# Spreading the small products of a graph layer over TensorE's four strips, with an earlier ranking and two slot buffers

## The chip, the cores and the metric

The kernel runs on one core of a Trainium2 chip. The metric is the device time of one execution in microseconds (us): before the change the median of three runs is 540.39 us (539.81 to 543.72). The engines are named as the profile names them: PE is TensorE (PEld its weight loads), ACT is ScalarE, DVE is VectorE, POOL is GpSimd, SP is SyncE, which here only issues DMAs. "The change" is the kernel after it; line numbers are those of the kernel before, unless said otherwise.

## The reference, cut to what matters

A graph layer with 6250 nodes of 128 features and 100000 edges, sorted by their target node. Each edge has one of two types, and its message is the source row times the weight of that type. The messages are summed per target; the node's own product is added; then relu, a residual and a layer norm.

```python
Xs = X[src]                                    # 100000 x 128
m_data = Xs @ W_data.T + b_data
m_ctrl = Xs @ W_control.T + b_control
msg = jnp.where((edge_types == 0)[:, None], m_data, m_ctrl)
agg = jax.ops.segment_sum(msg, dst, num_segments=X.shape[0])
out = jax.nn.relu(agg + (X @ W_self.T + b_self))
x = _layernorm(x + out, axis=-1)               # (h - mean) / sqrt(var + 1e-5)
```

## The kernel before

**Tiles.** The products of all nodes with both message weights are made once (49 blocks of 128 nodes, each with two types: 98 columns of a table). Each is held as three bf16 parts side by side, 384 columns (`D3`), in the tile `m3`, which stays in SBUF. The targets are cut into 39 *windows* of 160 nodes (`WN`); ten nodes are left over and go through an indirect gather. Eleven *groups* of windows (`GROUPS`: 1, 2, then nine of 4) share their preparation.

**Ranking** (`ranks`, once per group). The edges of a window (22 x 124 slots) are loaded (`win`) and turned into one-hot rows (`hots`). PE counts and ranks them (L810, L846), DVE reduces the ranks (`slot`, L851), PE scatters each edge into one of 32 places per table column (L890, into the PSUM tile `vt`). DVE takes `vt` out as `vs` (L905 to L911). SP writes `vs` to DRAM (`packed`, L917), from where each window of the group is read back, spread over all partitions (`rows`, 784 KB, L1043). Edges that find no place go through a short list (L993) and a gather.

**Sums** (`sums`, once per window). DVE turns `rows` in place into one-hot columns (L1053). Then 25 *groups of strips* follow each other, g = 0 to 24. Stage one (L1075): four products with 32 columns of weights each, so that each uses one strip of 32 columns of PE and writes 32 partitions of the PSUM tile `gp`; each streams 384 columns of `m3`. They fetch up to 128 message rows. ACT or DVE copies them out of PSUM to `gs` as bf16 (L484 or L485, the function `evict`). Stage two sums them by target into the PSUM tile `a`. A window has 160 targets: 128 of them are four blocks of 32, one strip each, and stream the 384 columns of `gs` (L1092). The last 32 targets go into the columns of `a` behind the first 384 (`a[..., D3:]`): there the three parts of 128 columns are three *small products* (L1095), the part c on strip c, so on strips 0, 1 and 2. At the window's end those three blocks are copied out as `bs` (96 partitions) and added by a product with `fold` (L615), a 96 x 32 matrix of three identities.

**Finish** (`close`, once per group). DVE adds the three parts of `a` (L624), the residual and the statistics; POOL or ACT scales; SP stores. The products of L615 go into the same PSUM tile `vt` that the scatter uses (it has one buffer), and DVE reads them at L633.

**Order.** Nothing is scheduled on the chip: each engine runs its list of instructions in order. A planner (`Plan.run`) writes these lists: it goes through all operations with assumed costs (the number in `add("PE", 0.168, ...)` is such a cost, in us) and gives each engine, when it is free, the ready operation with the earliest due time. It also decides there whether an `evict` goes to ACT or DVE. The due times of `ranks` follow from `when`, which for later groups lies `LEAD` = 80 ahead of the due time of the group's first window (`T0 + w0 * TW`, 13 per window). Buffers are rings: the load of `rows` of window i may only be issued when stage one of window i - 3 has read its buffer (`B(work, [P, R, NT], BF16, "rows", 3, ...)`). Before the windows, the first three chunks of the transposed input (`xts`) use the same three buffers.

Of the kernel before, what the change touches and what calls it, by code (L numbers as in the profile page):

```python
# [10 lines left out]
F32 = mybir.dt.float32  # L11
BF16 = mybir.dt.bfloat16
# [9 lines left out]
P = 128  # L22
D = 128
D3 = 3 * D
# [14 lines left out]
WN = 160  # L39
# [5 lines left out]
R = 32  # L45
W4 = WN - P
NT = 2 * NB
NS = 25
# [218 lines left out]
def sums_over_windows(ctx, tc, x, xt, edges, w, bias, out, total):  # L267
    nc = tc.nc
    V, A, G, T, S = nc.vector, nc.scalar, nc.gpsimd, nc.tensor, nc.sync
# [6 lines left out]
    add = plan.add  # L276
# [5 lines left out]
    def B(pool, shape, dtype, name, bufs=1, room=None):  # L282
        return Buf(plan, pool, shape, dtype, name, bufs, room)

    def C(shape, dtype, name):
        return Buf(plan, const, shape, dtype, name, 1)

    XC = 4 * WN
    T0 = 36.0
    DOUBLE = ('lo1', 'to1', 'slot2', 'pay', 'inside', 'unit')  # L290
    TW = 13.0
# [32 lines left out]
    def vec(due, cols, fn, r, w, rate=1.04):  # L324
        return add("DVE", dve(cols, rate), fn, due, r, w)

    def vp(on_pool, due, cols, fn, r, w, rate=1.04, slow=1.0):
# [57 lines left out]
    fold = C([3 * R, R], F32, "fold")  # L385
    vec(30, R, lambda: V.tensor_add(fold.t, ident.t[: 3 * R, 0:R], ident.t[: 3 * R, R : 2 * R]),
        [ident], [fold])
    vec(30, R, lambda: V.tensor_add(fold.t, fold.t, ident.t[: 3 * R, 2 * R : 3 * R]),
        [ident, fold], [fold])
# [115 lines left out]
    for j, n in enumerate(XB):  # L505
        ring = ("rows", 3, R * NT) if j < 3 else ("hot2", 2, NS * WN)
        xts.append(B(work, [D, 2 * n * P], BF16, *ring))
# [208 lines left out]
    def ranks(gi, w0, nw, when, late, step, engines):  # L716
# [140 lines left out]
        for ci, (k0, k1) in enumerate(zip(cs, cs[1:])):  # L857
# [36 lines left out]
            add("PE", .25 + m * 0.0275, scatter, dc + 1, [(two, 0), (two, 1)] + hkeys(k0, k1), [vt])  # L894
# [136 lines left out]

    def sums(gi, w0, nw, placed):
# [5 lines left out]
        for i in range(nw):  # L1038
            due = T0 + (w0 + i) * TW
            sp = B(work, [P, R, NT], BF16, "rows", 3, R * NT)  # L1040
# [27 lines left out]
            for g in range(NS):  # L1068
# [4 lines left out]
                def stage1(g=g, gp=gp, sp=sp, last=last):  # L1073
                    for t in range(2 if last else 4):
                        T.matmul(gp.t[R * t : R * t + R, :D3], sp.t[:, :, 4 * g + t],  # L1075
                                 m3.t[:, 4 * g + t, :], start=True, stop=True)
                s1.append(add("PE", 0.168, stage1, d, [sp] + m3_key(g), [gp]))
# [12 lines left out]
                def stage2(g=g, gs=gs, a=a, hot2=hot2, last=last):  # L1090
                    for j in range(4):
                        T.matmul(a.t[R * j : R * j + R, :D3], hot2.t[:, g, R * j : R * j + R],  # L1092
                                 gs.t, start=g == 0, stop=False, skip_group_check=True)
                    for c in range(3):
                        T.matmul(a.t[R * c : R * c + R, D3:], hot2.t[:, g, P:],  # L1095
                                 gs.t[:, c * D : (c + 1) * D], start=False, stop=last,
                                 skip_group_check=True)
                s2.append(add("PE", 0.178, stage2, d + 0.9, [gs, (hot2, sum(g >= c for c in cuts[1:-1]))], [a]))
# [6 lines left out]
            bs = B(work, [3 * R, D], F32, "bs", 5)  # L1105
            evict(lambda bs=bs: bs.t, lambda a=a: a.t[: 3 * R, D3:], D, due + TW + 0.8, [a], [bs]).slack = 0.25
# [86 lines left out]
    for gi, nw in enumerate(GROUPS):  # L1193
        if gi == 0:
            when, late, step, engines = 0.0, 12.0, 0.5, ["SP"]
        elif gi == 1:
            when, late, step, engines = 8.0, 14.0, 0.6, ["SP", "ACT"]
        else:
            span = nw * TW
            when = max(when + late + 22 * step + GAP, T0 + w0 * TW - LEAD)  # L1200
            late, step, engines = LF * span, SF * span, ["SP"]
        todo.append((gi, w0, nw, when, late, step, engines))
        w0 += nw
# [170 lines left out]
```

## Time and profile before

| | |
|---|---|
| median of three runs | 540.39 us (539.81 to 543.72) |
| the profiled execution | 542.22 us, its span 540.4 us |
| granted TensorE clock, mean | 0.983 |
| PE busy | 502.1 us (93%), 13288 products |
| PEld busy | 432.6 us (80%) |
| DVE busy | 441.1 us (82%) |
| ACT busy | 429.0 us (79%) |
| POOL busy | 201.5 us (37%) |

Three stretches make up the span: the message products until about 62 us, the 39 windows until about 528 us, and a tail that closes the last group. In the views, a line reads: source line, engine, operation, names of output and inputs (buffer numbers left out), shapes, count, then busy time and mean duration, then idle time of that engine before it and what ended it. Instructions of an engine overlap, so the union of their times is less than count times duration, and a busy PE is not PE at its peak. `g` and `x` are the PSUM tiles of stage one, `a` that of stage two.

### The profile page before, as it was taken

The page shows a single profiled execution, that of the slowest core. Times are in us where ns is not written, and L with a number is a line of the kernel's source. Part 1 is how long each engine was busy: PE and PEld are TensorE (multiplying, and loading weights), DVE is VectorE, ACT ScalarE, POOL GpSimd, SP SyncE. Part 2 cuts the span into 40 slices and gives each one's busy share as a digit, 9 for nine tenths or more (in the row PEclk, how much of TensorE's full clock was granted, in tenths as well). Part 3 has the DMA queues.
Part 4 walks back from the last instruction along what each step waited for, and adds up shares of the span by engine and source line. Part 5 has one row for each costly group of instructions (what it writes and reads, how often), then busy time and mean ns, then how long its engine had stood idle before and what let it go on. Part 6 is the DMA issues. An engine that isn't in the chain of part 4 may idle for free. (4 is left out here: it accounts for less than half of the span.)

```text
span 540.4 us, 30907 instructions
## 1 busy us (share of the span) xinstructions
PE 502.1 (93%) x13288; PEld 432.6 (80%) x13288; DVE 441.1 (82%) x1168; ACT 429.0 (79%) x1077; POOL 201.5 (37%) x284
## 2 busy tenths in 40 slices
PE   7799879799999988999999999999999999999991
PEld 4465557699889877888988887888898899888990
DVE  6388989889989997898989889979978678956642
ACT  4566767698889877888988878978898898878990
POOL 1000535700830684176067247707701720542000
PEclk9989899999999998999999999999999999999997
DMA  7466661540453055325413533351342352234200
GB/s 244 160 256 224 240 181 29 167 161 6 134 145 88 12 139 151 98 77 152 141 38 111 141 95 95 91 180 41 115 128 88 115 163 89 63 107 126 70 19 17
DMA packets 44932, 63.43 MB, mean 117 GB/s; under 512 B 19178, under 2 KB 35279, under 8 KB 44751
## 3 DMA queue, kind: packets, MB, share of 16 engines
q1 hardware_dynamic: 41745, 56.22, 33.5%
q0 software_dynamic: 1120, 2.23, 2.0%
q10 hardware_dynamic: 1922, 2.91, 1.7%
q8 instruction: 106, 1.74, 1.3%
q14 instruction: 39, 0.32, 0.2%
HBM read 45.61 MB, written 13.82 MB: 110 GB/s over the span
## 5 line engine op out<-in xcount | busy, mean ns | idle before, releaser
L1092 PE MATMUL a<-gs,hot 128*32 128x384 bf16 x3744 | 376.1, 328 | 0.4 <-issue 0.3
L484 ACT CAST gs<-g 128x384 bf16<-128x384 f32 x700 | 302.9, 492 | 64.3 <-PE g L1075 53.6
L1075 PE MATMUL g<-m,rows 128*32 128x384 bf16 x2958 | 327.1, 336 | 9.0 <-DVE rows L1053 5.7
L1075 PEld LDWEIGHTS <-rows 128*32 128x32 bf16 x3822 | 253.4, 134 | 27.7 <-DVE rows L1053 6.5
L1095 PE MATMUL a<-gs,hot 128*32 128x128 bf16 x2808 | 273.1, 220 | 2.1 <-issue 2.1
L1092 PEld LDWEIGHTS <-hot 128*32 128x32 bf16 x3900 | 206.4, 98 | 6.7 <-issue 3.1
L1095 PEld LDWEIGHTS <-hot 128*32 128x32 bf16 x2925 | 155.6, 97 | 14.1 <-issue 2.4
L1075 PE MATMUL x<-m,rows 128*32 128x384 bf16 x864 | 122.0, 335 | 0.0
L484 ACT CAST gs<-x 128x384 bf16<-128x384 f32 x199 | 98.3, 494 | 8.6 <-PE x L1075 5.7
L1061 DVE TENSOR_TENSOR hot<-iota_b,to_d 128x1920 bf16<-128x1920 bf16 (+2 forms) x85 | 93.1, 1105 | 0.1
L851 DVE TENSOR_REDUCE slot<-rk 124x8 f32<-124x400 f32 (+2 forms) x99 | 56.1, 567 | 22.3 <-PE g L1075 10.3
L674 POOL TENSOR_SCALAR xr<-xr,mv,rstd 128x128 f32<-128x128 f32 (+1 forms) x44 | 56.5, 1289 | 21.9 <-DVE rstd L651 18.4
L846 PE MATMUL rk<-hots,tri 128*32 128x400 bf16 (+1 forms) x388 | 51.3, 337 | 4.5 <-DVE slot L851 1.5
L1053 DVE TENSOR_SCALAR rows<-rows,pid 128x3136 bf16<-128x3136 bf16 (+1 forms) x46 | 41.6, 904 | 5.7 <-DMA rows<-packed 5.7
L937 POOL TENSOR_SCALAR pv<-slot 124x88 f32<-124x88 bf16 x9 | 9.5, 1058 | 79.6 <-DVE slot L868 74.2
L624 DVE TENSOR_REDUCE s<-a 128x128 f32<-128x384 f32 (+1 forms) x40 | 22.1, 551 | 15.7 <-ACT bs L484 9.9
L1016 POOL DMA_INDIRECT sr<-table,at x20 | 29.8, 1489 | 10.8 <-DVE at L1004 6.2
L491 POOL COPY to_d<-vs 32x100 bf16<-32x100 bf16 (+1 forms) x72 | 29.2, 406 | 5.9 <-DVE vs L911 2.7
L846 PEld LDWEIGHTS <-tri 128*32 128x32 bf16 x428 | 22.9, 96 | 9.9 <-issue 8.6
L803 DVE TENSOR_TENSOR hots<-hots,val 124x1200 bf16<-124x1200 bf16 (+3 forms) x42 | 28.0, 675 | 0.0
L799 DVE TENSOR_TENSOR hots<-iota_b,st 124x1200 bf16<-124x1200 bf16 (+3 forms) x42 | 27.6, 671 | 0.0
L767 POOL TENSOR_SCALAR pay<-u 124x88 f32<-124x88 f32 x9 | 8.9, 994 | 46.2 <-DVE u L752 45.1
(224 smaller groups left out, 667.9 us busy)
## 6 DMA issues: line engine op xcount, KB each, us to landing
rows<-packed SPq DMA_DIRECT2D x36, 784.0 KB
table<-m SPq DMA_DIRECT2D x12, 768.0 KB
xc<-in_xt SPq DMA_DIRECT2D x9, 320.0 KB
rows<-packed ACTq DMA_DIRECT2D x3, 784.0 KB
rows<-in_xt SPq DMA_DIRECT2D x8, 256.0 KB
xr<-in_x SPq DMA_DIRECT2D x8, 256.0 KB
out<-xr SPq DMA_DIRECT2D x8, 256.0 KB
gl<-sr SPq DMA_DIRECT2D x39, 48.0 KB
```

Source lines behind the costliest of these rows:

```text
L484: [("ACT", act(cols), lambda: A.copy(o(), src())), ("DVE", dve(cols), lambda: V.tensor_copy(o(), src()))], None, None, due, r, w, lat)
L491: "POOL", 0.25 + cols * 0.0014, lambda: G.tensor_copy(o(), src()), due, r, w)
L674: fp = lambda k=k, m=m: G.tensor_scalar(h.t[:m, k, :], h.t[:m, k, :], mv.t[:m, k, 0:1], rstd.t[:m, k : k + 1], op0=ALU.subtract, op1=ALU.mult)
L803: vec(when + 2 + pace * k0, m * NC, lambda k0=k0, k1=k1, hs4=hs4, hp=hp: V.tensor_tensor(hp(), hp(), fl(val)[:, k0 * nw : k1 * nw, None, : ...
L846: T.matmul(acc.t[R * j : R * j + R, : (k1 - k0) * wide], tri.t[:, R * j : R * j + R], flat(k0, k1, P), start=True, stop=True, skip_group_c ...
L851: vec(due, (k1 - k0) * wide, lambda k0=k0, k1=k1, acc=acc: V.tensor_reduce(slot.t[:, k0:k1, :], acc.t[:EP, : (k1 - k0) * wide].rearrange(" ...
L1016: add("POOL", GC, lambda pr=pr, sr=sr: G.indirect_dma_start(out=sr.t[: room(pr)], out_offset=None, in_=table[:, :], in_offset=bass.Indirec ...
L1053: add("DVE", dve(half * NT, 0.305) + 0.05, lambda sp=sp, rs=rs: V.tensor_scalar(sp.t[:, rs], sp.t[:, rs], pid1.t, None, op0=ALU.is_equal), ...
L1061: lambda i=i, hot2=hot2, s4=s4, c0=c0, c1=c1: V.tensor_tensor(hot2.t[:, c0:c1].rearrange("p g (c d) -> p g c d", d=2), iota1_b.t.rearrange ...
L1075: T.matmul(gp.t[R * t : R * t + R, :D3], sp.t[:, :, 4 * g + t], m3.t[:, 4 * g + t, :], start=True, stop=True)
L1092: T.matmul(a.t[R * j : R * j + R, :D3], hot2.t[:, g, R * j : R * j + R], gs.t, start=g == 0, stop=False, skip_group_check=True)
L1095: T.matmul(a.t[R * c : R * c + R, D3:], hot2.t[:, g, P:], gs.t[:, c * D : (c + 1) * D], start=False, stop=last, skip_group_check=True)
```

## The change

Four edits.

1. **Small products on four strips.** A counter of columns per strip (`load`) is kept while the program is written. The function `turn(n, cols)` takes the n strips with the least columns so far, in that order, and adds `cols` to each. Stage one takes its four strips in the order that `turn(4, D3)` gives, stage two does so too, and the three small products go to the strips of `turn(3, D)`: any three of the four, the one that had most columns left out. The sum of the last 32 targets is then spread over four blocks of partitions, so `bs` has 128 partitions and `fold` four identities (one more addition of 32 columns on DVE, once).
2. **Further ahead.** `when` of group gi lies 4 us per group number above 4 further ahead: 4 for group 5, up to 24 for group 10.
3. **Two buffers** for `rows` in place of three. The load of a window then waits for stage one of window i - 2. The third chunk of the transposed input gets a tile of its own (`x2`).
4. **Costs of the planner.** Stage one 0.163 in place of 0.168, stage two 0.204 in place of 0.178, scatter 0.2 + 0.016 m in place of 0.25 + 0.0275 m. They cost nothing by themselves; they move instructions.

```diff
-    fold = C([3 * R, R], F32, "fold")
+    fold = C([P, R], F32, "fold")
...
     for j, n in enumerate(XB):
-        ring = ("rows", 3, R * NT) if j < 3 else ("hot2", 2, NS * WN)
-        xts.append(B(work, [D, 2 * n * P], BF16, *ring))
+        if j == 2:
+            xts.append(C([D, 2 * n * P], BF16, "x2"))
+        else:
+            ring = ("rows", 2, R * NT) if j < 2 else ("hot2", 2, NS * WN)
+            xts.append(B(work, [D, 2 * n * P], BF16, *ring))
...
-            add("PE", .25 + m * 0.0275, scatter, dc + 1, [(two, 0), (two, 1)] + hkeys(k0, k1), [vt])
+            add("PE", .2 + m * 0.016, scatter, dc + 1, [(two, 0), (two, 1)] + hkeys(k0, k1), [vt])
...
+    load = [0] * 4
+
+    def turn(n, cols):
+
+        js = sorted(range(4), key=lambda j: (load[j], j))[:n]
+        for j in js:
+            load[j] += cols
+        return js
...
-            sp = B(work, [P, R, NT], BF16, "rows", 3, R * NT)
+            sp = B(work, [P, R, NT], BF16, "rows", 2, R * NT)
...
                 def stage1(g=g, gp=gp, sp=sp, last=last):
-                    for t in range(2 if last else 4):
+                    for t in (0, 1) if last else turn(4, D3):
                         T.matmul(gp.t[R * t : R * t + R, :D3], sp.t[:, :, 4 * g + t],
                                  m3.t[:, 4 * g + t, :], start=True, stop=True)
-                s1.append(add("PE", 0.168, stage1, d, [sp] + m3_key(g), [gp]))
+                s1.append(add("PE", 0.163, stage1, d, [sp] + m3_key(g), [gp]))
...
                 def stage2(g=g, gs=gs, a=a, hot2=hot2, last=last):
-                    for j in range(4):
+                    for j in turn(4, D3):
                         T.matmul(a.t[R * j : R * j + R, :D3], hot2.t[:, g, R * j : R * j + R],
                                  gs.t, start=g == 0, stop=False, skip_group_check=True)
-                    for c in range(3):
-                        T.matmul(a.t[R * c : R * c + R, D3:], hot2.t[:, g, P:],
-                                 gs.t[:, c * D : (c + 1) * D], start=False, stop=last,
+                    for c, j in enumerate(turn(3, D)):
+                        T.matmul(a.t[R * j : R * j + R, D3:], hot2.t[:, g, P:],
+                                 gs.t[:, c * D : (c + 1) * D], start=False, stop=g > NS - 3,
                                  skip_group_check=True)
-                s2.append(add("PE", 0.178, stage2, d + 0.9, [gs, (hot2, sum(g >= c for c in cuts[1:-1]))], [a]))
+                s2.append(add("PE", 0.204, stage2, d + 0.9, [gs, (hot2, sum(g >= c for c in cuts[1:-1]))], [a]))
...
-            bs = B(work, [3 * R, D], F32, "bs", 5)
-            evict(lambda bs=bs: bs.t, lambda a=a: a.t[: 3 * R, D3:], D, due + TW + 0.8, [a], [bs]).slack = 0.25
+            bs = B(work, [P, D], F32, "bs", 5)
+            evict(lambda bs=bs: bs.t, lambda a=a: a.t[:, D3:], D, due + TW + 0.8, [a], [bs]).slack = 0.25
...
-            when = max(when + late + 22 * step + GAP, T0 + w0 * TW - LEAD)
+            when = max(when + late + 22 * step + GAP, T0 + w0 * TW - LEAD - 4 * max(gi - 4, 0))
```

Two places show how the order moves. The first is SP's queue where the group of windows 19 to 22 gets its slots: the write of `packed`, the loads of `rows` that stand behind it, and what lies between. Before, the loads are those of windows 19, 20 and 21:

```order
L917 DMA packed<-vs 128x2x98
L1043 DMA rows<-packed 128x3136
L607 DMA xb<-in_xt 128x4x32
L1043 DMA rows<-packed 128x3136
L830 DMA past<-csb 64x2x200
L833 DMA hots<-past 4x4400
L1023 DMA gl<-sr 64x384 x2
L1043 DMA rows<-packed 128x3136
```

In the change the loads are those of windows 18, 19 and 20:

```order
L921 DMA packed<-vs 128x2x98
L1056 DMA rows<-packed 128x3136
L834 DMA past<-csb 64x2x200
L837 DMA hots<-past 4x4400
L1056 DMA rows<-packed 128x3136
L611 DMA xb<-in_xt 128x4x32
L1027 DMA gl<-sr 64x384 x4
L1056 DMA rows<-packed 128x3136
```

Before, the first load behind the write reads what was just written; now a load of the group before stands between, so the write has come forward by a window against the loads. Each load now also stands behind more of the small DMAs of the ranking (`past`, `hots`, `gl`), and waits for a buffer that comes free one window later.

The second place is DVE's list where the scatter of that same group is taken out of `vt`. Before (`xr<-vt,xr` at L633 reads the products with `fold` from the same PSUM tile):

```order
L905 TENSOR_SCALAR vst<-vt 128x2x49
L982 TENSOR_SCALAR fi<-ci 124x32
L908 SCALAR_TENSOR_TENSOR vs<-vst,vt 128x98
L911 TENSOR_SCALAR vs<-vst 128x98
L982 TENSOR_SCALAR fi<-ci 124x32 x2
L633 SCALAR_TENSOR_TENSOR xr<-s,xr 128x128
L1061 TENSOR_TENSOR hot_9186<-iota_b,to_d 128x1920
L633 SCALAR_TENSOR_TENSOR xr<-vt,xr 128x128
```

In the change:

```order
L909 TENSOR_SCALAR vst<-vt 128x2x49
L952 TENSOR_REDUCE n8b<-fl_9000 124x4
L912 SCALAR_TENSOR_TENSOR vs<-vst,vt 128x98
L915 TENSOR_SCALAR vs<-vst 128x98
L986 TENSOR_SCALAR fi<-ci 124x32 x3
L1074 TENSOR_TENSOR hot_8800<-iota_b,to_d 128x1920
L969 COPY pos_all<-vt 124x4
L744 SCALAR_TENSOR_TENSOR inside,counts<-rel,low 124x88
```

The read of the fold products, which stood seven rows behind the scatter's, has moved away: it now comes 22 rows behind, after the short list of the group has gone through `vt` too. On PE the fold products accordingly stand two groups of strips behind the list's products (L993) instead of three behind the scatter.

More of the change, by code (lines that the diff above doesn't have):

```diff
@@ L384, in sums_over_windows @@
     vec(2, R, lambda: V.memset(later.t[:, R:], 1.0), [], [(later, 1)], 0.3)
-    fold = C([3 * R, R], F32, "fold")
-    vec(30, R, lambda: V.tensor_add(fold.t, ident.t[: 3 * R, 0:R], ident.t[: 3 * R, R : 2 * R]),
+    fold = C([P, R], F32, "fold")
+    vec(30, R, lambda: V.tensor_add(fold.t, ident.t[:, 0:R], ident.t[:, R : 2 * R]),
         [ident], [fold])
-    vec(30, R, lambda: V.tensor_add(fold.t, fold.t, ident.t[: 3 * R, 2 * R : 3 * R]),
-        [ident, fold], [fold])
+    for j in (2, 3):
+        vec(30, R, lambda j=j: V.tensor_add(fold.t, fold.t, ident.t[:, R * j : R * j + R]),
+            [ident, fold], [fold])
     minus = C([P, P], BF16, "minus")
```

## The prediction

> **What bounds the kernel now.** I read the busy times by stretch first. Columns: length, then busy time of PE, PEld, DVE, ACT, POOL, the granted clock and the DMA share.
>
> ```profile
> 62.00:110.00 48.00, 40.84 (x1103) 33.91 (x1099) 42.79 (x129) 34.47 (x89) 24.30 (x31) 0.97 0.45 127
> 110.00:160.00 50.00, 49.63 (x1451) 45.80 (x1445) 46.98 (x118) 43.43 (x112) 17.12 (x28) 1.00 0.36 111
> 160.00:210.00 50.00, 46.39 (x1318) 41.71 (x1313) 46.36 (x109) 39.34 (x101) 25.43 (x35) 0.97 0.38 102
> ...
> 310.00:360.00 50.00, 47.74 (x1382) 41.70 (x1376) 43.70 (x108) 41.36 (x107) 26.33 (x30) 1.00 0.34 102
> ...
> 410.00:460.00 50.00, 49.78 (x1466) 45.86 (x1460) 38.40 (x87) 43.28 (x112) 15.57 (x23) 1.00 0.33 101
> ...
> sum 466.00, PE 448.71 PEld 400.22 DVE 393.57 ACT 389.98 POOL 192.57; mean PE 49.86 PEld 44.47 DVE 43.73 ACT 43.33 POOL 21.40
> ```
>
> From 62 to 528 us the 39 windows run, 11.9 us each (466 / 39). PE stands still for 466 - 448.7 = 17.3 us of it, and most of that lies in three stretches (7.2 before 110, 3.6 before 210, 2.3 before 360). DVE has 72 us to spare in all, but only 3.0 in 110 to 160; ACT has 6.6 there. So PE is the bound, with two engines close behind. A busy PE need not stream at its best, so the second view is the time line of PE inside a window; "x3" are three products that follow each other.
>
> ```profile
> 300.77 0.39 PE L1092 MATMUL a<-gs,hot 128*32 128x384 bf16 x4
> 300.93 0.33 PE L1075 MATMUL g<-m,rows 128*32 128x384 bf16 x1
> 300.98 0.24 PE L1095 MATMUL a<-gs,hot 128*32 128x128 bf16 x3
> 301.04 0.34 PE L1075 MATMUL g<-m,rows 128*32 128x384 bf16 x3
> ...
> 301.26 0.33 PE L1075 MATMUL g<-m,rows 128*32 128x384 bf16 x1
> 301.36 0.24 PE L1095 MATMUL a<-gs,hot 128*32 128x128 bf16 x3
> ...
> 301.58 0.33 PE L1075 MATMUL g<-m,rows 128*32 128x384 bf16 x1
> ...
> 301.75 0.23 PE L1095 MATMUL a<-gs,hot 128*32 128x128 bf16 x3
> ```
>
> This is the strips at work. The single L1075 is the fourth strip's: it starts before the three small products (300.93 against 300.98) although it stands behind them in the list, and comes again after 0.33 and 0.32 us (300.93, 301.26, 301.58). It has no small product. The other three strips come round after 0.38 and 0.39 us (300.98, 301.36, 301.75): 384 columns in about 0.16 us (300.77 to 300.93), the small product in 0.06 (300.98 to 301.04), and 384 again. Each strip streams without a hole; the fourth runs ahead of the others until what it needs is not there yet. So the three strips with a small product set the pace, at 0.385 us a group.
>
> **The change part by part.** The span is 540.4 us; the profiled execution took 542.2, inside the runs shown and 1.8 over their median, 540.39. I sum against the span and set the result against the median, since the two are alike.
>
> *Small products on four strips.* The weight loads of L1095 have all their records:
>
> ```profile
> L1095 PEld LDWEIGHTS <-hot 128*32 128x32 bf16 x2925 | 155.6, 97 | 14.1 <-issue 2.4
> ```
>
> 2925 / 3 = 975 groups. A strip bears 0.75 of a small product per group in place of 1. By the starts on one strip a small product costs 0.055 us (a third of 0.16 is 0.053, the starts show 0.06), so a group takes 0.25 x 0.055 = 0.0138 less on the strips that set the pace: 975 x 0.0138 = **13.4 us** (12.2 to 14.6 by the starts' rounding and by the last groups, where stage one uses two strips). No product is added. What goes along: `bs` is copied with 128 partitions in place of 96, and DVE makes one more short addition before the windows. A copy of 384 columns took 475 ns with 64 partitions and 492 with 128:
>
> ```profile
> L484 ACT CAST gl<-g 64x384 bf16<-64x384 f32 x34 | 16.2, 475 | 0.9 <-PE g L1075 0.9
> L484 ACT CAST gs<-g 128x384 bf16<-128x384 f32 x700 | 302.9, 492 | 64.3 <-PE g L1075 53.6 <-PE rk L846 1.6 <-PE vt L960 1.2
> ```
>
> 17 ns for 64 partitions makes under 0.4 us over 39 windows, on an engine that waits for PE: nothing.
>
> *The copies out of PSUM.* Once PE is quicker, ACT is next. Its copies overlap:
>
> ```profile
> 502.10 1.25 ACT L484 CAST gs<-g 128x384 bf16<-128x384 f32 x3
> 503.24 0.49 ACT L484 CAST gs<-x 128x384 bf16<-128x384 f32 x1
> ```
>
> Three take 1.25 and one 0.49, so they follow each other after (1.25 - 0.49) / 2 = 0.38 us. PE's group comes down from 0.385 to 0.371, below that. The change also gives ACT more of them: by the order DVE's `gs` and `gl` copies fall from 42 to 23. Where PE has other work between (own products, ranking, scatter), ACT catches up: a window has 25 copies, 9.5 us, and takes 11.9 now. Only the last four windows, with no ranking left, are pure: 100 groups x 0.009 is 0.9. I add **1 us** (0 to 13.4, all of the gain, if ACT paced every group). The page "TensorEngine Tiling (Array Packing)" of the Trainium skill, under Performance Considerations, warns of this: tiling makes TensorE quicker but not the emptying of PSUM, which may become the bottleneck, and it advises both ScalarE and VectorE for it, where this change leans on one. By that rule the first term would be about 0; the trace so far bears it out only in part, with ACT at 43.4 us of 50 in the fullest stretch.
>
> *Ranking further ahead, and the planner's costs.* PE's waits:
>
> ```profile
> PE g L1075 <- DVE rows L1053: 5.7, 3, 3.2
> PE g L1075 <- ACT gs L484: 2.9, 4, 1.6
> PE vt L615 <- DVE vs L908: 2.1, 3, 0.8
> PE rk L846 <- DVE slot L851: 1.5, 2, 1.3
> ```
>
> The longest, 3.2 us, is at the start of window 11:
>
> ```profile
> 195.52 1.91 SPq L1043 DMA_DIRECT2D rows<-packed  x2
> 202.74 1.03 DVE L1053 TENSOR_SCALAR rows<-rows,pid 128x3136 bf16<-128x3136 bf16 x1
> ```
>
> The slots of window 11 were asked for too late. In PE's order 29 groups stood between the end of that group's scatter and the window's first product; now there are 43, so the write has 14 x 0.385 = 5.4 us more. That covers the stall: **-3.2** (0 to -3.2). The earlier groups' stalls (7.2 us before 110) have unchanged lead and stay. The fold products waited three times behind the scatter for `vt`, 2.1 us; they now stand as close behind the list's products, which DVE also must take out first, so half of it may come back: **-1** (0 to -2.1). The rest of the order, in both directions, I take as 0 (-6 to +4: PE's remaining idle time after 110, about 6 us, bounds the gain).
>
> *Two buffers.* How loads and buffers stand now (the issues of SP, its waits and DVE's, then one load and its use):
>
> ```profile
> rows<-packed SPq DMA_DIRECT2D x36, 784.0 KB
> ```
> ```profile
> SPq L1043 <- PE g L1075: 84.2, 23, 9.2
> ```
> ```profile
> DVE rows L1053 <- DMA rows<-packed: 5.7, 5, 2.8
> ```
> ```profile
> 350.90 0.58 SPq L1043 DMA_DIRECT2D rows<-packed  x1
> ```
> ```profile
> 355.80 1.04 DVE L1053 TENSOR_SCALAR rows<-rows,pid 128x3136 bf16<-128x3136 bf16 x1 [2.84 <-DMA rows<-packed]
> ```
>
> 23 loads already leave when a buffer comes free, so nearly every load will now leave a window later. It needs 4.9 us (350.90 to 355.80) and DVE 1.04; the next window begins a window's length after the buffer is free, 10.5 to 11.9 us. That leaves 4 to 6 us, which covers the load. But DVE's instruction stands in its list where the load should just have landed, no longer a window later; a late load holds up all of DVE: the `slot` reduces, hence the ranking on PE, the one-hot tiles of stage two (L1061) and the statistics. At 355.8 it did: DVE stood 2.84 us, and PE 1.3 for `slot`. On SP, behind the waiting load, are `past`, `hots`, `gl` and the next loads of edges; these have a window or more to spare with the longer lead. I take two or three such cases, **+3** (0 to 36 x 1.3 = 47 if each of SP's 36 loads did it).
>
> Sum: -13.4 + 1 - 3.2 - 1 + 3 = -13.6. 540.4 - 13.6 = 526.8, so **527 us** (522 to 533 with the near ends of the terms).
>
> **The rivals.**
>
> *The quicker case*: no load comes late, ACT keeps up, the `vt` waits go whole, and with costs nearer to PE's real pace the new order also spares the 6 us of other waits after 110: 540.4 - 13.4 - 3.2 - 2.1 - 6 = 516. For it: the planner took 0.346 us a group for one that takes 0.385, and takes 0.367 now for one of 0.371, so its order fits the chip better. Against: DVE gets little slack in the dense stretches.
>
> *ACT becomes the bound*: groups go at ACT's 0.38 and the first term is lost: 540.4 - 3.2 - 1 + 3 = 539. For it: 0.38 against 0.371. Against: ACT is idle 13% in the fullest stretch, and a strip's work in a window is more than the 25 groups. The skill's PSUM rule above would give this time.
>
> *Slower, by the buffers*: DVE waits for landings, and PE for DVE, as at 355.8, at two of three loads: 24 x 1.3 = 31, so 540.4 - 13.4 + 1 - 3.2 - 1 + 31 = 555. It decides from (13.6 + 3) / 1.3 = 13 late loads on. For it: 5 waits of DVE for these loads even with three buffers (5.7 us in all). Against: loads no longer run two at a time, as at 195.52, so each lands sooner.
>
> *The change doesn't do what it says*: the products don't share the strips as counted, because an instruction whose strip is busy holds up those behind it in the list: again only the order's terms, 539. Against: the fourth strip does run ahead today.
>
> **How the numbers follow.** Chances: forecast 0.54, quicker 0.19, ACT the bound 0.12, buffers 0.08, strips not as counted 0.07. The time is that of the forecast, 527. The range reaches from the quicker case, 516, to just short of the 539 of the two cases without the first term: 516 to 537; it leaves out these and the buffers' case, partly, some 2 in 10. A measurement of this kernel tells about 1% (5.4 us) from no change. Faster by more than that, below 535, are the first two cases and part of the third: 0.78. Within 1%: the rest of the third and the fifth, 0.14. Slower: 0.08.
>
> **What would show it.** In the profile after: right, if L1095's successor on each strip follows the same pace, so that the four strips alternate in carrying two or three full and one small product and a group's mean period in a full stretch is near 0.37; if the wait of L1075 for `rows` near window 11 is gone; if `DVE rows <- DMA rows<-packed` is a handful of waits. Wrong, if ACT's `gs` copies show no idle time before them and PE waits for `gs` in tens of us; if the `rows` waits of DVE come at most windows and PE's idle time in the dense stretches grows past 1 us per window; or if a group's period stays at 0.38.

## The result, and the profile after

The change makes the kernel a little slower: 543.26 us (median; 540.5 to 549.0) against 540.37 us for the kernel before on the same chip, a ratio of **1.007** (95% interval 1.0053 to 1.0086). Forecast were 527 us and a range of 516 to 537. The profiled execution after took 545.8 us, 2.5 over its median, with a span of 543.9 us and a mean granted clock of 0.976 (0.983 before). Line numbers of the kernel after lie 4 higher in the ranking, 13 higher in the windows.

The windows of the kernel after, for the stretches that the prediction shows of before (length, then busy time of PE, PEld, DVE, ACT, POOL, the granted clock, DMA share and rate):

```profile
62.00:110.00 48.00, 40.83 (x1003) 31.51 (x999) 41.72 (x123) 31.30 (x78) 19.57 (x31) 0.88 0.34 98
110.00:160.00 50.00, 49.33 (x1481) 45.37 (x1473) 46.77 (x118) 44.58 (x119) 20.80 (x30) 1.00 0.33 104
160.00:210.00 50.00, 47.76 (x1431) 42.83 (x1427) 46.52 (x114) 43.12 (x113) 25.35 (x36) 1.00 0.41 114
...
310.00:360.00 50.00, 46.54 (x1339) 40.28 (x1335) 43.17 (x113) 41.00 (x106) 26.87 (x36) 1.00 0.33 108
...
410.00:460.00 50.00, 49.26 (x1480) 44.71 (x1474) 38.58 (x95) 44.70 (x114) 18.51 (x34) 1.00 0.34 102
...
sum 466.00, PE 442.34 PEld 389.42 DVE 382.58 ACT 392.44 POOL 189.80; mean PE 49.15 PEld 43.27 DVE 42.51 ACT 43.60 POOL 21.09
```

Where PE is full (110 to 160, 410 to 460), it does 1481 and 1480 products in 50 us instead of 1451 and 1466: the strips do more. From 160 to 210 it does more as well (1431 instead of 1318), without the stall at window 11. In the other stretches shown it gives this back. In the first 48 us it has done 1003 products instead of 1103, in as much busy time, with a granted clock of 0.88 instead of 0.97; and over the 466 us it stands still for 23.7 (before: 17.3). The first product of stage two of window 1 starts at 84.9 us instead of 80.5: 4.4 us, more than the whole loss, are gone by then, and what follows gains and loses about as much.

The time line of PE in the kernel after, inside a window:

```profile
300.62 0.24 PE L1108 MATMUL a<-gs,hot 128*32 128x128 bf16 x3
...
300.97 0.27 PE L1108 MATMUL a<-gs,hot 128*32 128x128 bf16 x3
...
301.34 0.26 PE L1108 MATMUL a<-gs,hot 128*32 128x128 bf16 x3
```

The small products come round after 0.35 and 0.37 us. Before, it was 0.38 and 0.39. Over the whole run, where one group follows the other directly (periods of 0.30 to 0.45 us, some 700 of the 975 groups), the mean period falls from 0.380 to 0.370 us. So the strips share the work as meant.

The waits of the kernel after that answer to those of the prediction, and the two longest of DVE:

```profile
DVE s L628 <- PE a L1108: 22.0, 8, 4.3
DVE slot L855 <- PE rk L850: 21.2, 28, 4.1
...
PE vt L997 <- DVE hr L978: 4.6, 5, 1.4
...
PE g L1088 <- DVE rows L1066: 3.5, 2, 2.1
...
PE a L1105 <- issue: 3.1, 8, 1.0
...
PE a L1108 <- issue: 2.7, 5, 1.5
...
PE g L1088 <- ACT gs L485: 1.8, 3, 1.4
...
DVE rows L1066 <- DMA rows<-packed: 0.9, 1, 0.9
```

Of the two of DVE, the wait for PE at `s` is new in this size (before: 5.7 us, at three lines of PE). At `slot` DVE waited as long before, 21.6 us, which the view then put down to three lines of PE. No single wait explains the time: what was feared of the two buffers (DVE waiting for landings) is 0.9 us, what was feared of ACT (PE waiting for `gs`) is 1.8, less than the 2.9 before.

### The profile page after: what moved, and what is told of

It is laid out like the page before. It is cut to its first block, busy times and chain, and to the rows that moved or that the text cites. A ratio compares the mean times of both kernels' runs of the same rounds, so it can differ in the third digit from the quotient of the medians.

```text
span 543.9 us, 30925 instructions
## 1 busy us (share of the span) xinstructions
PE 498.7 (92%) x13288; PEld 424.2 (78%) x13288; DVE 431.1 (79%) x1150; ACT 433.8 (80%) x1096; POOL 196.2 (36%) x284
## 3 DMA queue, kind: packets, MB, share of 16 engines
q8 instruction: 106, 1.74, 1.3%
## 4 chain that ended last, share of the span: by engine, by line
PE 53%; POOL 8%; DVE 7%; issue 3%; DMA 2%; ACT 1%; DVEq 0%; SPq 0%; ACTq 0%; POOLq 0%
PE a L1105 20%; PE g L1088 17%; PE x L1088 5%; POOL to_d L492 4%; PE a L1108 4%; PE rk L850 2%; PE a L585 1%; DVE hr L978 1%; PE vt L894 1%; DVE hot L1074 1%; DMA xr<-in_x 1%; DMA hots<-past 1%; DVE slot L855 1%; PE vt L997 1%; POOL pv L941 1%
## 5 line engine op out<-in xcount | busy, mean ns | idle before, releaser
L1105 PE MATMUL a<-gs,hot 128*32 128x384 bf16 x3744 | 356.3, 328 | 3.4 <-issue 3.1
L1088 PE MATMUL g<-m,rows 128*32 128x384 bf16 x2958 | 297.1, 334 | 6.7 <-DVE rows L1066 3.5
L1088 PEld LDWEIGHTS <-rows 128*32 128x32 bf16 x3822 | 264.6, 135 | 25.5 <-issue 11.5
L1105 PEld LDWEIGHTS <-hot 128*32 128x32 bf16 x3900 | 171.8, 98 | 12.3 <-issue 7.0
L1108 PEld LDWEIGHTS <-hot 128*32 128x32 bf16 x2925 | 150.3, 97 | 15.6 <-issue 2.9
L485 ACT CAST gs<-x 128x384 bf16<-128x384 f32 x214 | 111.5, 521 | 9.5 <-PE x L1088 7.4
L1088 PE MATMUL x<-m,rows 128*32 128x384 bf16 x864 | 89.7, 330 | 0.6 <-ACT gs L485 0.4
L678 POOL TENSOR_SCALAR xr<-xr,mv,rstd 128x128 f32<-128x128 f32 (+1 forms) x44 | 49.6, 1134 | 39.9 <-DVE rstd L655 39.6
L850 PE MATMUL rk<-hots,tri 128*32 128x400 bf16 (+1 forms) x388 | 39.8, 337 | 5.0 <-DMA hots<-past 2.1
L492 POOL COPY to_d<-vs 32x100 bf16<-32x100 bf16 (+1 forms) x72 | 36.5, 507 | 7.3 <-POOL ci L983 2.3
L1020 POOL DMA_INDIRECT sr<-table,at x20 | 23.2, 1158 | 17.0 <-DVE slot L872 11.4
```

The lines of the kernel that those rows point to most:

```text
L485: [("ACT", act(cols), lambda: A.copy(o(), src())), ("DVE", dve(cols), lambda: V.tensor_copy(o(), src()))], None, None, due, r, w, lat)
L492: "POOL", 0.25 + cols * 0.0014, lambda: G.tensor_copy(o(), src()), due, r, w)
L678: fp = lambda k=k, m=m: G.tensor_scalar(h.t[:m, k, :], h.t[:m, k, :], mv.t[:m, k, 0:1], rstd.t[:m, k : k + 1], op0=ALU.subtract, op1=ALU.mult)
L850: T.matmul(acc.t[R * j : R * j + R, : (k1 - k0) * wide], tri.t[:, R * j : R * j + R], flat(k0, k1, P), start=True, stop=True, skip_group_c ...
L1108: T.matmul(a.t[R * j : R * j + R, D3:], hot2.t[:, g, P:], gs.t[:, c * D : (c + 1) * D], start=False, stop=g > NS - 3, skip_group_check=True)
```

## The experiments

All ratios are against the kernel before, run beside it, with 95% intervals. The runs come from several chips, on which the kernel before takes 537.6 to 541.4 us, so the ratios can be compared and the times can't; where an expectation is in us, the ratio times 540.4 is set against it. "Old costs" are the planner's numbers of the kernel before, "new costs" those of the one after.

### One edit alone, one edit undone

**e1** is the kernel before with the first edit alone: `fold`, `bs`, `turn` and the order of the strips.

```diff
-    fold = C([3 * R, R], F32, "fold")
+    fold = C([P, R], F32, "fold")
...
-                    for c in range(3):
+                    for c, j in enumerate(turn(3, D)):
...
-            bs = B(work, [3 * R, D], F32, "bs", 5)
+            bs = B(work, [P, D], F32, "bs", 5)
```

> Only the spread of the small products is put into the kernel before (with fold and bs for four strips); buffers, lead and the planner's costs stay, so the order of all engines stays too. Theory A (the strips' gain is real, and the new order gives it back): 540.4 less 8 to 13, so 527 to 532. Rival B (the strips never set the pace, ACT or the waits do): within 2 us of before, 538 to 542. Rival C (the spread itself hurts, since strips that all carry the same have no slack left): over 542.

Measured: 535.02 us, **0.9944** (0.992 to 0.9969). The gain is 3 us of the 13.4. In terms of 540.4 this is 537.4, between theory A and rival B: neither is right.

**e2**, **e3** and **e4** undo one edit of the kernel after each: e2 has three buffers, e3 the old lead, e4 the old costs.

```diff
-            sp = B(work, [P, R, NT], BF16, "rows", 2, R * NT)
+            sp = B(work, [P, R, NT], BF16, "rows", 3, R * NT)
```

> The changed kernel with three buffers for rows in place of two. If the two buffers give the gain back (SP stands for a buffer at nearly every load, 167 us in 30 waits against 84 in 23): 543.3 less 8 to 14, so 529 to 535. If the costs or the lead do: within 3 us of the change, 540 to 546.

Measured: 539.78 us, 1.0042 (1.0016 to 1.0067), within 3 us of the change, as the second case has it.

```diff
-            when = max(when + late + 22 * step + GAP, T0 + w0 * TW - LEAD - 4 * max(gi - 4, 0))
+            when = max(when + late + 22 * step + GAP, T0 + w0 * TW - LEAD)
```

> The changed kernel with the old lead of the ranking. If the longer lead crowds DVE, POOL and PE in the dense stretch, 210 to 410 us, it gains 4 to 10: 533 to 539. If the lead is what keeps the loads in time, it loses: 545 to 552. If it plays no part: 541 to 545.

Measured: 541.47 us, 1.0065 (1.0034 to 1.0096): in this order the lead plays no part.

```diff
-            add("PE", .2 + m * 0.016, scatter, dc + 1, [(two, 0), (two, 1)] + hkeys(k0, k1), [vt])
+            add("PE", .25 + m * 0.0275, scatter, dc + 1, [(two, 0), (two, 1)] + hkeys(k0, k1), [vt])
...
-                s1.append(add("PE", 0.163, stage1, d, [sp] + m3_key(g), [gp]))
+                s1.append(add("PE", 0.168, stage1, d, [sp] + m3_key(g), [gp]))
...
-                s2.append(add("PE", 0.204, stage2, d + 0.9, [gs, (hot2, sum(g >= c for c in cuts[1:-1]))], [a]))
+                s2.append(add("PE", 0.178, stage2, d + 0.9, [gs, (hot2, sum(g >= c for c in cuts[1:-1]))], [a]))
```

> The changed kernel with the planner's old costs (stage one 0.168, stage two 0.178, the old scatter). If the new costs write an order in which DVE asks PE too early (DVE's waits for PE: s 22.0 us and slot 21.2, against 3.2 and 20 before), it gains 5 to 13: 530 to 538. If the buffers or the lead are the cause: 541 to 546.

Measured: 528.66 us, **0.9814** (0.9782 to 0.9847). In these two orders the edit that the prediction took as 0 carries the result: without it the kernel is 1.9% faster than before, with it 0.7% slower. Whether the costs as such do this, or only the order that they happened to give, these two runs can't tell.

The next four combine the lines of these diffs. **e5** has the old stage costs and the new scatter cost, **e6** the kernel before with two buffers and the longer lead alone, **e7** the old costs with three buffers, **e8** the old costs with the old lead.

> The changed kernel with the old costs of the two stages alone (0.168 and 0.178), the new cost of the scatter kept. Theory: the stages' costs write the order that gives the gain back, since they set the planned pace of all 975 groups: as the run with all old costs, 526 to 532. Rival: the scatter's cost does (it is the one that was changed most, from 1.57 to 0.97 us for 48 products, where the trace has 0.87): as the change, 540 to 546. Both in part: 533 to 539.

> The kernel before with two buffers and the longer lead alone: small products on three strips, old costs. Against the run with the spread and these two and the old costs (528.7) it gives what the spread is worth in that order. Theory (the spread is worth its 13 us where PE's waits don't stand in the way; with the order of before two thirds of it went into a longer wait for window 1 and window 11 and half clock after it): 538 to 542. Rival (the spread is worth 3 us in any order, and the other two edits are what brought 7): 530 to 533.

> Spread, longer lead and old costs, with three buffers. Theory (two buffers help the start: windows 1 and 2 are then not loaded at the same time, 5.8 us to landing in place of 8.5): 532 to 536. Rival (two buffers cost, the lead brings the gain): 524 to 528.

> Spread, two buffers and old costs, with the old lead. If the longer lead plays no part here either: 526 to 531. If it brought the gain over the spread alone (535.0): 533 to 537.

Measured: e5 533.48 us, 0.9889 (0.9842 to 0.9936); e6 534.02 us, 0.9925 (0.9886 to 0.9964); e7 540.11 us, 1.0033 (0.9999 to 1.0067); e8 529.88 us, 0.9849 (0.9804 to 0.9894). In terms of 540.4, e5 (534.4) is "both in part", e6 (536.3) and e8 (532.2) lie between their two cases, and e7 (542.2) is slower than either of its own. Read as sums, this would say that two buffers gain 2.2% under the old costs (e7 to e4) and nothing under the new ones (e2 to the kernel after), and that the lead is worth nothing. The next runs show that such differences may not be read as sums.

### Two theories on the costs, and both forecasts fail

With the new costs DVE gets 23 of the copies out of PSUM in place of 42. Theory "copies": ACT, left alone with them, is what loses the time. Theory "pace": a PE that is planned slower gets fewer groups between a request and the use of its answer. **e9** gives DVE its 42 copies back under the new costs, **e10** takes them away under the old ones, both by ACT's planned cost of a copy (0.392 in e9, 0.35 in e10; 0.378 elsewhere); **e12** has the old scatter cost and plans a still quicker PE. The diffs of e9 and of e12's stages:

```diff
-        [("ACT", act(cols), lambda: A.copy(o(), src())),
+        [("ACT", 0.392 if cols == D3 else act(cols), lambda: A.copy(o(), src())),
```
```diff
-                s1.append(add("PE", 0.163, stage1, d, [sp] + m3_key(g), [gp]))
+                s1.append(add("PE", 0.158, stage1, d, [sp] + m3_key(g), [gp]))
...
-                s2.append(add("PE", 0.204, stage2, d + 0.9, [gs, (hot2, sum(g >= c for c in cuts[1:-1]))], [a]))
+                s2.append(add("PE", 0.168, stage2, d + 0.9, [gs, (hot2, sum(g >= c for c in cuts[1:-1]))], [a]))
```

> The kernel after, with ACT's copy of 384 columns planned at 0.392 us in place of 0.378: DVE's share of the copies of stage one is 42 again, as in the kernel before (23 in the kernel after). Theory 'copies' (the dearer stage costs hurt because they leave ACT alone with the copies): the 1.8% between the kernel after and the one with the old stage costs comes back, ratio 0.985 to 0.993. Theory 'pace' (they hurt because a PE that is planned slower gets fewer groups between a request to another engine and the use of its answer): nothing comes back, 1.000 to 1.010.

> The kernel after with the old planner costs, and ACT's copy of 384 columns planned at 0.350 us in place of 0.378: DVE's share of the copies falls from 41 to 18. Theory 'copies': it loses what the stage costs lost, ratio 0.995 to 1.005. Theory 'pace': it stays where the kernel with the old costs was, 0.977 to 0.987.

> The kernel after with the old scatter cost and stage costs of 0.158 and 0.168 us, so 0.326 a group planned (0.346 in the kernel before, 0.367 in the one after); DVE gets 60 of the copies. Theory 'pace': more groups between request and use, so no worse than with the old costs, 0.970 to 0.984. If the old costs were at an optimum, or DVE cannot carry 19 copies more: 0.984 to 1.000. Theory 'copies' alone: at or below 0.981, as ACT is relieved further.

Measured: e9 550.84 us, **1.0164** (1.0124 to 1.0205); e10 546.16 us, **1.0078** (1.0047 to 1.011); e12 534.95 us, 0.9878 (0.9847 to 0.9909). The forecast of "copies" fails in e9, which should have won 1.8% and lost 0.9%; that of "pace" fails in e10, which should have kept 0.981, and in e12, which should have come to 0.984 or less. (e10 ends just above what "copies" gave it, 0.995 to 1.005; e12 fits its second case, 0.984 to 1.000.) Each of these runs also has an order of its own, and the runs further below show that this alone is worth up to 2.8%; so a small effect of the copies or of the pace isn't excluded. Much of what e9 lost can be seen in one place. Its longest wait of PE, the time line of that wait, DVE's of the same moment, and the stretches of 3.4 us around it:

```profile
PE rk L850 <- DVE slot L855: 5.2, 1, 5.2
```
```profile
167.59 0.52 PE L850 MATMUL rk<-hots,tri 128*32 128x400 bf16 x4 [5.24 <-DVE slot L855]
```
```profile
166.01 1.04 DVE L1066 TENSOR_SCALAR rows<-rows,pid 128x3136 bf16<-128x3136 bf16 x1 [5.70 <-DMA rows<-packed]
```
```profile
161.20:164.60 3.40, 1.15 (x36) 0.92 (x25) 0.00 (x0) 1.59 (x5) 0.00 (x0) 1.00 0.58 206
164.60:168.00 3.40, 0.41 (x8) 0.26 (x11) 1.99 (x6) 0.00 (x0) 0.23 (x1) 0.51 0.96 321
168.00:171.40 3.40, 3.40 (x56) 2.88 (x52) 2.37 (x7) 1.91 (x6) 2.15 (x4) 0.50 0.59 199
171.40:174.80 3.40, 3.40 (x118) 3.08 (x112) 3.40 (x6) 3.36 (x10) 0.00 (x0) 0.99 0.09 18
```

Four products of the ranking wait 5.24 us for DVE's `slot`, everything behind them waits too, and then PE runs at half its clock for another 3.4 us. DVE is late because it stands 5.70 us for a load of `rows`, which SP issued only at 161.34. This is the mechanism of the prediction's slower rival (DVE waits for a landing, and PE for DVE), here in a single load. In the kernel after PE waits for `slot` 1.8 us in all. ACT's planned cost of a copy was changed, and a new wait came up at a DMA, on DVE and on PE.

### The spread, on one and the same order

**e11** is the kernel after without the spread, and closes the square.

> The kernel before with two buffers, the longer lead and the new planner costs, small products on three strips. It completes the square: no spread with old costs was 0.9925, spread with old costs 0.9814, spread with new costs 1.007. If the costs hurt by themselves, whatever PE's real pace: 1.013 to 1.023 and the spread is worth 1% here too. If they hurt because the planned pace (0.367 us a group) leaves no margin to the real one (0.368 with the spread, 0.381 without): less of a loss, 0.995 to 1.008, and the spread is worth nothing under the new costs.

Measured: 551.23 us, **1.0188** (1.0157 to 1.0219), in the range of "the costs hurt by themselves". The spread itself does not move the order: in each of the three pairs the engines' lists name the same operations in the same places, but for the one addition of `fold`. So these pairs measure it without a change of order (the second and third by ratios from different chips):

| order | without the spread | with it | gain | PE busy | span less PE busy |
|---|---|---|---|---|---|
| of the kernel before | 1 | 0.9944 (e1) | 0.6%, 3.0 us | 502.1 to 494.5 | 38.3 to 41.1 |
| two buffers, lead, old costs | 0.9925 (e6) | 0.9814 (e4) | 1.1%, 6.0 us | 498.6 to 490.0 | 31.7 to 39.0 |
| of the kernel after | 1.0188 (e11) | 1.007 (after) | 1.2%, 6.4 us | 506.1 to 498.7 | 40.5 to 45.2 |

(Gains by the ratios, times 540.4; by the intervals they are good to about 1.3, 2.7 and 1.9 us. The last two columns from the first lines of each page, one execution each, which scatters by some 3 us.) PE's busy time falls by 7.4 to 8.6 us, not by 13.4, and 2.8 to 7.3 of that come back as standstill. The first part can be read off the starts of the small products: in each pair some 700 of the 975 groups follow another directly, and their mean period falls by 0.0103 to 0.0108 us, 7 to 8 us in all. For the second part the order of the kernel before shows where it arises: this is the start of window 1, the kernel before and then e1, PE's time line.

```profile
78.89 0.71 PE L1075 MATMUL g<-m,rows 128*32 128x384 bf16 x12 [2.25 <-DVE rows L1053]
```
```profile
78.61 1.18 PE L1085 MATMUL g<-m,rows 128*32 128x384 bf16 x12 [4.67 <-DVE rows L1063]
```

The windows of e1, of which the stretch of this wait and the sum:

```profile
62.00:110.00 48.00, 40.67 (x1047) 32.66 (x1043) 40.92 (x118) 32.61 (x82) 22.46 (x30) 0.88 0.37 111
...
sum 466.00, PE 440.62 PEld 396.42 DVE 394.72 ACT 389.12 POOL 191.89; mean PE 440.62 PEld 396.42 DVE 394.72 ACT 389.12 POOL 191.89
```

In e1 PE is done with window 0 earlier, and waits for the same slots until almost the same moment: 4.67 us in place of 2.25. The longer standstill brings the half clock as well: the twelve products behind it take 1.18 us in place of 0.71, the granted clock of the stretch is 0.88 in place of 0.97, and from 62 to 110 us e1 does 1047 products, where the kernel before does 1103. A quicker PE meets the chains of slots, ranks and copies, which do not get quicker.

### How much a planner's number is worth at all

Left were two theories. "Values": the old stage costs are good numbers and the new ones bad. "Draw": any change of a cost deals the order anew, and the waits fall by chance. Six runs move one planned cost by 0.002 us, half a per cent of a planned group, and nothing else.

**n1** and **n2** do so to the kernel after with the old costs (0.170 and 0.166 in place of 0.168), **n3** and **n4** to the kernel after (0.165 and 0.161 in place of 0.163), **b1** and **b2** to the kernel before (0.170 and 0.166 in place of 0.168). The whole edit of b1:

```diff
-                s1.append(add("PE", 0.168, stage1, d, [sp] + m3_key(g), [gp]))
+                s1.append(add("PE", 0.170, stage1, d, [sp] + m3_key(g), [gp]))
```

> The kernel after with the old planner costs, but stage one planned at 0.170 us in place of 0.168. Theory 'values': within 0.4% of the kernel with the old costs, 0.977 to 0.986. Theory 'draw' (each change of a cost deals a new order, whose waits fall by chance): anywhere from 0.975 to 1.010, away from 0.981 by 0.5% or more in at least two of these four runs.

> The kernel after with the old planner costs, but stage one planned at 0.166 us in place of 0.168. Theory 'values': 0.977 to 0.986. Theory 'draw': anywhere from 0.975 to 1.010.

> The kernel after with stage one planned at 0.165 us in place of 0.163. Theory 'values': within 0.4% of the kernel after, 1.003 to 1.011. Theory 'draw': anywhere from 0.985 to 1.015.

> The kernel after with stage one planned at 0.161 us in place of 0.163. Theory 'values': 1.003 to 1.011. Theory 'draw': anywhere from 0.985 to 1.015.

> The kernel before with stage one planned at 0.170 us in place of 0.168, nothing else. If the order of the kernel before is a lucky draw among its neighbours: 1.005 to 1.015. If it is an ordinary one: 0.993 to 1.005, as often below 1 as above.

> The kernel before with stage one planned at 0.166 us in place of 0.168, nothing else. Lucky draw: 1.005 to 1.015. Ordinary: 0.993 to 1.005.

| family | stage one 0.002 lower | as it is | 0.002 higher | mean |
|---|---|---|---|---|
| kernel before | 1.005 (1.0021 to 1.0078) | 1 | 1.0284 (1.0235 to 1.0333) | 1.011 |
| kernel after | 0.9951 (0.992 to 0.9981) | 1.007 (1.0053 to 1.0086) | 0.9936 (0.9906 to 0.9966) | 0.999 |
| after with old costs | 0.9834 (0.9785 to 0.9882) | 0.9814 (0.9782 to 0.9847) | 0.9901 (0.9868 to 0.9933) | 0.985 |

The draw is real: 0.002 us moves the time by 0.5 to 2.8% in five of the six runs, beyond the intervals, and by 0.2%, within them, in n2. "Values" had allowed 0.4%: n1, n3 and n4 leave its ranges, n2 keeps to them. b1 is slower than either of its cases, and b2 lies where the two meet. Part of the draw falls early: the first product of stage two of window 1 starts at 84.9 us in the kernel after, and at 81.0 and 80.5 in n3 and n4. Both neighbours of the kernel after are faster than it, and faster than the kernel before; both neighbours of the kernel before are slower than it. The comparison that was predicted sets the best of three orders against the worst of three. By the means of the families the whole change would be worth -1.2% (0.999 / 1.011), and without the new costs -2.6%. "Values" isn't refuted, though: the old-cost family (0.981 to 0.990) lies below the new-cost family (0.994 to 1.007), 1.4% apart by the means, though the intervals of the nearest two touch. Three orders each are too few to tell how much of that is the values, and the middle runs of the two lower rows come from other chips than their neighbours (the first row is from one). That stays open, and so do the effects of the buffers and of the lead, whose runs differ in order too.

The fastest version run is e4, at 0.9814; its neighbours say that the kind of kernel is worth 0.981 to 0.990, and where in this range a version falls is the draw.

## Why the prediction was wrong, point by point

**The spread (-13.4): the mechanism right, the size wrong.** Where groups follow each other directly, the mean period came down from 0.380 to 0.370 us, near to what was computed (0.385 to 0.371). The step that failed is "975 x 0.0138 = 13.4" taken whole into the span. In an order that does not move, it measured 3.0, 6.0 and 6.4 us: PE's busy time fell by 8, and part of that turned into longer waits. The prediction had seen that DVE has only 3.0 us to spare in 110 to 160 and that the stalls of 7.2 us before 110 "stay"; the stalls did not stay, they grew, since PE came to them sooner while what it waits for came when it came. Of the 5 us of busy time that are missing, about 2 are the smaller saving in these 700 groups (0.0105 in place of 0.0138 us each). The rest belongs to the other 270 or so, which come after other work, after a wait or at half clock; what the sharing is worth there isn't shown.

**The copies (+1, and the rival at 539).** Not seen. This is the group of ACT's copies after:

```profile
L485 ACT CAST gs<-g 128x384 bf16<-128x384 f32 x700 | 304.6, 510 | 62.8 <-PE g L1088 52.0
```

ACT still waits 52.0 us for PE in them (53.6 before), and PE 1.8 us for `gs`. The page "TensorEngine Tiling (Array Packing)" of the Trainium skill (Performance Considerations), by whose PSUM rule the gain would go to zero there, isn't borne out: the gain shrank for other reasons, and giving copies back to DVE did not help in the one order in which it was run (e9).

**Window 11 (-3.2) and `vt` (-1).** The wait at window 11 is gone: the 3.5 us in the list above lie at 61 and 83 us. The fold products' wait for `vt` fell from 2.1 to 0.5, but the list's products, which write the same tile, wait 4.6 us instead of 1.4 for their operand `hr` from DVE. Such terms are right or wrong by one place of one order, and the next order has other places.

**The rest of the order (0, -6 to +4): the step that failed most.** "They cost nothing by themselves; they move instructions" was true, and the bound on what moving is worth was not. Its upper end had no row behind it at all; its lower one, PE's remaining idle time, bounds a gain in the present list, not a loss in another. The three edits without the spread measure +10.2 us (e11; 8.5 to 11.8), where their terms in the sum come to -3.2 - 1 + 3 + 0 = -1.2. With the 6.4 us of the spread this is the result: a little slower instead of 13.6 faster. The new costs make +2.6% between the orders at hand (e4 to the kernel after, and e6 to e11 with the spread out), 14 us, but 1.4% by the means of the families, and 0.002 us alone makes up to +2.8%. So some of the 10.2 is the draw: the kernel after lies 0.8% above the mean of its family, the kernel before 1.1% below that of its own. How much is left for the edits themselves, three orders can't tell. That the time came out slower at all, and not a little faster as n3 and n4 did, is bad luck of this order; that it came out far from -13.6 is not, as far as three orders tell. The argument of the quicker case, that costs nearer to PE's real pace make an order that fits better, isn't borne out: of the two families, three orders each, the one with the more accurate costs is the slower.

**Two buffers (+3, and the rival at 555).** DVE waited 0.9 us for landings, less than before (5.7). In this order the sum's +3 and the rival fall. In others their mechanism is there: e9 stood 5.7 us for one late load, and e3, with the old lead, has 11.0 us of such waits. The rival's "against" came out in the early windows of e4: with two buffers the second load leaves later, and the first one no longer leaves beside it. The issue on ACT's queue and DVE's use in e4, 5.8 us apart; the second load leaves 4.9 us after the first:

```profile
67.36 0.35 ACTq L1056 DMA_DIRECT2D rows<-packed  x1
...
72.25 0.37 SPq L1056 DMA_DIRECT2D rows<-packed  x1
...
73.16 0.62 DVE L1066 TENSOR_SCALAR rows<-rows,pid 128x1568 bf16<-128x1568 bf16 x1
```

and in the kernel before, where the loads of windows 1 and 2 leave together, 7.4:

```profile
70.20 0.37 SPq L1043 DMA_DIRECT2D rows<-packed  x1
70.21 0.37 ACTq L1043 DMA_DIRECT2D rows<-packed  x1
...
77.61 0.63 DVE L1053 TENSOR_SCALAR rows<-rows,pid 128x1568 bf16<-128x1568 bf16 x1 [0.83 <-DMA rows<-packed]
```

In e7, which is e4 with three buffers, the two leave together as well, and DVE starts 8.3 us later (68.04 to 76.29). In the kernel after it starts 7.4 us after the load (73.29 to 80.66), but without having waited for it.

**The chances.** All three signs that the prediction named for being right came true: the period near 0.37, no wait at window 11, and a handful of waits of DVE for landings. They test the terms that the sum had, and the time went wrong beside them. A 0.08 for slower came from naming one mechanism for it, when the largest risk was the part that the trace of before could not price: the new order as a whole.

## What to carry to other kernels

Where a planner writes the order, an edit of one of its numbers is a new draw: here half a per cent of a planned cost moved the time by up to 2.8%, so a comparison of two such kernels says little below that until each has been run with a few neighbouring numbers, and a kernel kept because it was the fastest of many has its luck in its time. To price an edit, hold the order fixed (as e1 with the kernel before, e6 with e4, and e11 with the kernel after do), and do not take a saving on the busiest engine whole into the span when other engines stand close behind it: here 3 to 6 us of 13 stayed. A change to a plan needs a range for the order itself in the forecast, to both sides.

## What the runs showed of the chip that was not expected

**The half clock sets in after a partly idle stretch.** In the kernel after, four stretches of 3.4 us around a wait at window 1 (the columns as in the windows above):

```profile
77.20:80.60 3.40, 1.74 (x35) 0.82 (x33) 3.40 (x9) 0.85 (x2) 0.24 (x1) 0.99 0.68 212
80.60:84.00 3.40, 1.79 (x20) 0.73 (x23) 3.40 (x6) 0.62 (x2) 0.79 (x1) 0.50 0.54 176
84.00:87.40 3.40, 3.40 (x81) 2.51 (x84) 2.89 (x6) 1.51 (x4) 0.00 (x0) 0.50 0.14 34
87.40:90.80 3.40, 3.40 (x110) 3.08 (x106) 2.91 (x9) 2.83 (x8) 1.69 (x2) 1.00 0.02 5
```

PE was busy for 1.74 us of the first, with no wait above 1.42 us anywhere near; the clock then fell to 0.50 for two stretches, the second of them with PE busy throughout. So several short waits close together bring it on as a long one does, and a stretch of 3.4 us at half clock, if PE is busy throughout, costs 1.7 us besides the waits. The page "TensorE: Matmul & The Clock Gate" of the Trainium skill (Part 1) gives the window as about 3.4 us, which the lengths here agree with, and says that an idle window brings the low clock; here a window in which PE was busy half of the time did too. Not each such window does: in the kernel before, PE was busy for 1.65 us of the stretch from 75.00 to 78.40 us, and the clock stayed at 1.00 in the next. So the busy time alone doesn't decide, and what else does isn't shown.

**PE stands still with nothing to wait for.** In the kernel after, PE's time line:

```profile
259.29 0.22 PE L1108 MATMUL a<-gs,hot 128*32 128x128 bf16 x1 [1.45 <-issue]
...
357.47 0.34 PE L1105 MATMUL a<-gs,hot 128*32 128x384 bf16 x3 [1.00 <-issue]
```

The trace shows nothing that PE waits for at these places. A DMA queue that carries instructions moves 106 packets in each of these kernels:

```profile
q8 instruction: 106, 1.74, 1.3%
```

At both places one of its packets ended just before (from 256.92 to 257.87, and from 355.25 to 356.21), and most other such gaps also lie behind one. That PE has run out of instructions there fits, but no run tested it, and with 106 packets in some 540 us one is seldom far from any moment. With a quicker PE they grow: between 56 and 530 us the waits of PE put down to "issue" go from 2.4 to 5.6, from 3.7 to 8.5 and from 6.5 to 9.0 us in the three pairs of one order.
